# Column filtering in all chunks of layer 2 but the first of an image, with what makes room for it, in a two-layer convolution kernel

## The chip, the cores and the metric

The kernel runs on one core of a Trainium2 chip. The metric is the time of one execution on the device in microseconds (us); times of the kernel before are the median of three runs. The engines of the core are named as the profile names them: PE (TensorE; PEld are its weight loads), DVE (VectorE), ACT (ScalarE), POOL (GpSimd) and SP (SyncE, which here only issues transfers). Sixteen DMA engines move data; SP and ACT issue on hardware queues (q1 and q10 in the profile), POOL on a software queue (q0). L685 means line 685 of the kernel before.

## The reference

Two layers of the same form on x of shape (8, 32, 252, 252): group normalization (16 groups of two channels), a 5 by 5 convolution with reflect padding (written with FFTs), and the input added to it.

```
def _L0_conv_ref(x, weight):
    xp = jnp.pad(x, ((0, 0), (0, 0), (p, p), (p, p)), mode='reflect')
    wp = wp.at[:, :, :k, :k].set(weight)
    wp = jnp.roll(wp, shift=(shift, shift), axis=(-2, -1))
    out_fft = jnp.einsum('bihw,oihw->bohw', jnp.fft.fft2(xp), jnp.fft.fft2(wp))
    return jnp.fft.ifft2(out_fft).real[:, :, p:-p, p:-p]
...
x = x + _L0_conv_ref(_gn(x), L0_conv_weight)
x = x + _L1_conv_ref(_gn(x), L1_conv_weight)
```

The statistics of the second normalization are those of the first layer's whole image, so layer 2 of an image can begin only when layer 1 of it is done. All data are float32.

## The kernel before, in words

**Layout.** The 128 partitions hold 32 channels times two column parities times two row parities (`quad`), so that a 5 by 5 filter becomes a 3 by 3 filter over blocks of 2 by 2 pixels, and one 128 by 128 matrix product does all 32 channels and four parities at once. The residual addition is folded into the weights (`add_residual`), the normalization into weights and one bias.

**Row filtering (always).** Along rows a Winograd scheme is used: four output rows come from six "points". `transform` makes the inputs of the points on DVE: `v` holds sums of a row and the row two below (`row_pairs`, or for layer 2 `row_sums`, see below), `u` holds 4 times a row plus another (`row_quads`, `last_rows`); from `u` come points 2 and 1, from `v` points 4 and 3 and, with `points05` (L609), points 0 and 5. `conv` multiplies: each point takes three products of up to 128x508 (`product`, L685), one for each column tap. A float32 product shows as two records in the trace. Afterwards ACT and DVE combine the points (`seed`, `evacuate`, `first_pair`, `difference`, `inner`, `parts05`, `outer`): `inner` writes output rows 1 and 2 of each group of four to a tile y, and the "outer" rows 0 and 3 come from points 0 and 5.

**Column filtering (some chunks).** For points 0 and 5 the three products can be replaced by a second scheme along the columns: DVE makes sums and differences of neighbouring columns (`columns`, L618 to L628), PE does eight products of half the width (`column_product`, L707), ACT seeds one bank from another (`seed_columns`, L711), and DVE adds up (`column_parts`, L792 to L794). `by_columns` (L969) says which chunks do so: in layer 1 nearly all from image 1 on, in layer 2 chunks 1, 2, 3, 5 and 7 of images 0 to 5, chunks 1, 2, 3 of image 6 and 1 to 5 of image 7.

**Order of the work.** An image is eight chunks of 16 block rows. After the first image of layer 1 the list `order` takes in turn a chunk of layer 1 of image b + 1 and a chunk of layer 2 of image b; each has a slot of PE time. Where a chunk has no columns, its six products of points 0 and 5 are done in the next slot. Nothing is scheduled by a tool: each step is entered with a time in `at`, the table is sorted by these times, and each engine executes its instructions in that order. The times only set the order.

**Layer 2's inputs.** In layer 2 the sums v are made by transfers and not by DVE (`row_sums`, L557 to L560): POOL issues a copy of the chunk y to v (1032 KB), waits for it to land, and issues two accumulating transfers (903 KB and 129 KB) on the same queue. The tile v (tag "va") has one buffer, so the next copy waits until `points05` has read v.

**Other transfers.** SP loads chunks of x (`load`; most chunks are loaded for one column parity and copied on ACT by `even_columns`; the last chunk of an image and chunk 1 are loaded for both, four transfers of about 0.5 MB), loads pieces of the next image for its statistics (`load_piece`, two buffers, loaded two pieces ahead; ACT sums them in `piece_sums`, L235 and L241), and writes the output. For the output ACT first interleaves the two column parities from y into a tile o (`store`, L925), half a chunk at a time, then SP sends the rows (L910). Reflected border columns of layer 1's y are written by ACT (`reflect`, L869 to L872). POOL writes the borders of x (`borders`).

Of the kernel before, what the change touches and what calls it, by code (L numbers as in the profile page):

```python
# [42 lines left out]
F32 = mybir.dt.float32  # L43
# [6 lines left out]
P = 128  # L50
Q = 32
# [5 lines left out]
def tile_conv_preact_x2(ctx: ExitStack, tc: tile.TileContext, x: bass.AP, w0: bass.AP, w1: bass.AP, out: bass.AP):  # L57
# [17 lines left out]
    xpool = ctx.enter_context(tc.tile_pool(name="xpool", bufs=2))  # L75
    spool = ctx.enter_context(tc.tile_pool(name="spool", bufs=2))
    ypool = ctx.enter_context(tc.tile_pool(name="ypool", bufs=9))
# [167 lines left out]
    def load_piece(b: int, i: int):  # L245
        src = x[b].rearrange("ch h w -> (ch h w)").rearrange("(p n) -> p n", p=P)
        if b == 0:
            t = ypool.tile([P, PIECE], F32, tag="y", name=f"st_{b}_{i}")
        else:
            t = spool.tile([P, PIECE], F32, tag="st", name=f"st_{b}_{i}")  # L250
        parts = 3 if (b, i) == (0, NPIECE - 1) else 1
        m = PIECE // parts
        for j in range(parts):
            S.dma_start(t[:, j * m : (j + 1) * m], src[:, i * PIECE + j * m : i * PIECE + (j + 1) * m])
        pieces[b, i] = t
# [281 lines left out]
    def transform(t0: float, t1: float, b: int, l: int, c: int, free: float = -100.0, now=(0, 0, 0)):  # L537

        wi = WIN[l]
        got = {}  # L540
        sent = l == 1 and (b, c) != (0, 0)

        def source():
# [5 lines left out]
        def row_sums(add: bool):  # L549

            t, nxt = source()
            if not add:

                i = max(order.index((b, l, c)) - order.index((B - 2, 1, NCH - 2)), 0)
                got["v"] = vpool.tile([P, ROWS, wi], F32, tag=("va", "v")[i % 2], name=f"v_{b}_{l}_{c}")
                got["vt"] = got["v"].rearrange("p (t i) w -> p t i w", i=4)
                G.dma_start(got["v"], t)  # L557
            else:
                G.dma_start(got["v"][:, 0 : ROWS - 2], t[:, 2:ROWS], accum_op=ALU.add)  # L559
                G.dma_start(got["v"][:, ROWS - 2 : ROWS], nxt[:, 0:2], accum_op=ALU.add)  # L560

        def row_pairs(j0: int = 0, j1: int = NT):
# [49 lines left out]
        def columns():  # L612

            t, (m, mo) = ts[b, l, c][2], evens_odds(l)
            sd = vpool.tile([P, 2, NT, 2, m], F32, tag="sdiff", name=f"sdiff_{b}_{l}_{c}")
            d = tpool.tile([P, NT, 2, 2, m], F32, tag="t05", name=f"d05_{b}_{l}_{c}")
            odd, even = t[:, :, :, 1 : 2 * m : 2], t[:, :, :, 2 : 2 * m + 1 : 2]
            V.tensor_add(sd[:, 0], odd, even)  # L618
            V.tensor_sub(sd[:, 1], even, odd)
            if m == mo:  # L620
                f = "p t e (m a) -> p (t e) a m"
                V.tensor_sub(
                    d.rearrange("p t e a m -> p (t e) a m"),
                    t[:, :, :, 0 : 2 * m].rearrange(f, a=2), t[:, :, :, 2 : 2 * m + 2].rearrange(f, a=2),
                )
            else:
                V.tensor_sub(d[:, :, :, 0], t[:, :, :, 0 : 2 * m : 2], t[:, :, :, 2 : 2 * m + 1 : 2])
                V.tensor_sub(d[:, :, :, 1, 0:mo], odd[:, :, :, 0:mo], t[:, :, :, 3 : 2 * mo + 2 : 2])  # L628
            ts[b, l, c][2] = d, sd
# [14 lines left out]
        else:  # L644
            if sent:
                two = begin(order.index((b, l, c)) - 2)
                at(two + 1.45, row_sums, False)
                at(two + 8.4, row_sums, True)
            else:
                at(t0, row_pairs)  # L650
            for dt, fn in ((2, row_quads), (3.2, last_rows), (3.6, point2)):
                at(t0 + dt, fn)
            at(max(t0 + 4.2, free + 9.45) if sent else t0 + 4.2, point4)
# [7 lines left out]
    def conv(b: int, l: int, c: int, t0: float, t1: float, t2: float = 0.0, j0: int = 0, j1: int = NT, m05=None, later: float = 10.2):  # L661
# [28 lines left out]
        def half(tile_, i: int, e: slice, m: int):  # L690

            return tile_[:, e, i * nt * ne : i * nt * ne + nt * m].rearrange("p e (t w) -> p e t w", t=nt)

# [66 lines left out]
        def parts05():  # L760
# [3 lines left out]
            stt(to[1], sd[:, 2], 8.0, sd[:, 1], ALU.mult, ALU.add)  # L764

        def outer(e: int):

# [19 lines left out]
        def column_parts():  # L787
# [4 lines left out]
            V.tensor_add(half(sums05, 0, both, ne), m12, even)  # L792
            V.tensor_sub(odd, m2[:, :, :, 0:no], odd)
            V.tensor_sub(half(sums05, 1, both, no), odd, m12[:, :, :, 0:no])  # L794

# [20 lines left out]
        if columns:  # L816
# [6 lines left out]
            for i in range(2):  # L823
                at(t2 + 0.05, outer_columns, i)
        elif m05:
# [5 lines left out]
        else:  # L831
            at(t1 + 1.5, parts05)
            at(t2 + 0.05, outer, 0)
            at(t2 + 0.05, outer, 1)
        if nt < NT:
# [3 lines left out]
        else:  # L839
            store(t1 + 1.5 if m05 else t2 + 0.7, b, c, got)  # L840


    def keep(t1: float, t2, b: int, c: int, got):
# [18 lines left out]
        def reflect():  # L862
            lo, hi = (1 if c == 0 else 0), (ROWS - 1 if c == NCH - 1 else ROWS)
            y, copy, r = got["y"], A.copy, slice(lo, hi)

# [47 lines left out]

    def store(t0: float, b: int, c: int, got):

        end = (b, c) == (B - 1, NCH - 2)
        copy = V.tensor_copy if end else A.copy

        def interleave(h: int, s: int):
            if s == 0:  # L920
                pool, tag = (spool, "st") if end else (opool, "o")
                got["o", h] = pool.tile([P, 4, 2 * WOUT[1]], F32, tag=tag, name=f"o_{b}_{c}_{h}")
            r, m = 8 * h + 4 * s, (3 if (c, h, s) == (NCH - 1, 1, 1) else 4)
            for cp in range(2):
                copy(got["o", h][halves[s], 0:m, cp::2], got["y"][halves[cp], r : r + m, :])  # L925

        def send(h: int):
            got["o"] = got.pop(("o", h))
            for s in range(2):
                send_rows(b, c, h, s, got, (G, G) if end else (S, S))  # L930

        for i, t in enumerate((0, 3.3, 5.8, 7.8)):
            at(t0 + t, interleave, i // 2, i % 2)
        at(t0 + 4.6, send, 0)
        at(t0 + 9.1, send, 1)


    def store_half(t0: float, b: int, c: int, h: int, got):
        def interleave(s: int, rows: slice, engines):
            if (s, rows.start) == (0, 1):  # L940
                got["o"] = opool.tile([P, 4, 2 * WOUT[1]], F32, tag="o", name=f"o_{b}_{c}_{h}")
            for cp in range(2):
                dst, src = got["o"][halves[s], rows, cp::2], got["y"][halves[cp], 4 * s : 4 * s + 4][:, rows]
                eng = engines[cp]
# [24 lines left out]
    def by_columns(b: int, l: int, c: int) -> bool:  # L969
        if l == 0:  # L970
            return c < NCH - 1 and (b > 1 or (b == 1 and c > 1))
        return c in {B - 1: (1, 2, 3, 4, 5), B - 2: (1, 2, 3)}.get(b, (1, 2, 3, 5, 7))

# [62 lines left out]
    for i, (b, l, c) in enumerate(order):  # L1036
# [36 lines left out]
        if l == 0 and b + 1 < B:  # L1073
            wide = 1 if b == 0 else 2
            if c == 0:
                for j in range(2):
                    at(begin(i - 1) + 1.0 if b > 1 else t0 + (8.0 if b else 1.0), load_piece, b + 1, j)
            if c < NPIECE // 2:
                for j in range(2):
# [4 lines left out]
                    at(t, piece_sums, b + 1, p)  # L1084
                    if p + 2 < NPIECE:
                        at(t + 2.6, load_piece, b + 1, p + 2)
            if c == 2:
# [49 lines left out]
```

## Time and profile before

| | us |
|---|---|
| median of three runs (1878.82 to 1884.2) | 1880.79 |
| the profiled execution | 1879.27 |
| its span, first to last instruction | 1877.5 |
| PE busy | 1839.2 |
| DVE busy | 1731.2 |
| ACT busy | 1493.8 |
| POOL busy | 396.2 |
| an image in the steady stretch (846.4 to 1071.6 of the span) | 225.2 |

How to read the lines that follow. A line of the groups gives line, engine, operation, output and inputs, shapes, count, then total busy time and the mean duration in ns of one, then the idle time before them with who ended it. A line of the windows gives start and end of a stretch, its length, the busy time of PE, PEld, DVE, ACT and POOL in it (with the number of instructions), the clock granted to PE (1.00 is full), the busy share of the DMA engines and what they moved in GB/s. A line of a timeline gives start, duration, engine, line, operation and tiles, and in brackets idle time just before it and what ended that. A line of the chain gives start, length, and the engine and line. A line of the DMA issues gives the tiles, the queue, the count, the size of one and the median time from issue to landing. The granted clock was 0.994 over the execution.

### The profile page before, as it was taken

The page shows a single profiled execution, that of the slowest core. Times are in us where ns is not written, and L with a number is a line of the kernel's source. Part 1 is how long each engine was busy: PE and PEld are TensorE (multiplying, and loading weights), DVE is VectorE, ACT ScalarE, POOL GpSimd, SP SyncE. Part 2 cuts the span into 40 slices and gives each one's busy share as a digit, 9 for nine tenths or more (in the row PEclk, how much of TensorE's full clock was granted, in tenths as well). Part 3 has the DMA queues.
Part 4 walks back from the last instruction along what each step waited for, and adds up shares of the span by engine and source line. Part 5 has one row for each costly group of instructions (what it writes and reads, how often), then busy time and mean ns, then how long its engine had stood idle before and what let it go on. Part 6 is the DMA issues. An engine that isn't in the chain of part 4 may idle for free.

```text
span 1877.5 us, 20381 instructions
## 1 busy us (share of the span) xinstructions
PE 1839.2 (98%) x5194; PEld 966.0 (51%) x5194; DVE 1731.2 (92%) x3030; ACT 1493.8 (80%) x2781; POOL 396.2 (21%) x855
## 2 busy tenths in 40 slices
PE   5999999999999999999999999999999999999998
PEld 4444455545555555555555455554555555555455
DVE  7988799999999999999999899999999999997796
ACT  5886788878887888888898798987898876765575
POOL 4543111131112211122111311113111141110211
PEclk8999999999999999999999999999999999999999
DMA  9877578878888877987878967888878866775785
GB/s 275 203 179 180 151 209 199 210 194 202 217 202 219 194 209 192 221 223 173 220 193 206 235 175 205 205 204 204 212 202 198 214 165 140 179 174 148 195 212 125
DMA packets 207110, 369.07 MB, mean 197 GB/s; under 512 B 19088, under 2 KB 173968, under 8 KB 196752
## 3 DMA queue, kind: packets, MB, share of 16 engines
q1 hardware_dynamic: 178832, 230.73, 49.8%
q0 software_dynamic: 27600, 134.20, 29.3%
q10 hardware_dynamic: 560, 2.83, 0.4%
q8 instruction: 41, 0.67, 0.2%
q14 instruction: 77, 0.63, 0.1%
HBM read 167.15 MB, written 67.39 MB: 125 GB/s over the span
## 4 chain that ended last, share of the span: by engine, by line
PE 80%; DVE 7%; DMA 6%; ACT 3%; issue 3%; SPq 0%; POOL 0%; DVEq 0%; ACTq 0%; POOLq 0%
PE m L685 28%; PE pairs L685 28%; PE sums L707 7%; PE extra L707 6%; PE sums L685 6%; PE extra L685 4%; DMA v<-y 2%; DMA st<-in_x_dram 1%; DMA v<-ytail 1%; DMA xs<-in_x_dram 1%; ACT o L925 1%; DVE sd L748 1%; DVE t L609 1%; DMA wraw<-in_L_conv_weight_dram 1%; DMA out_dram<-o 0%
## 5 line engine op out<-in xcount | busy, mean ns | idle before, releaser
L685 PE MATMUL pairs<-t,u 128*128 128x504 f32 (+2 forms) x1548 | 692.9, 586 | 5.4 <-ACT pairs L729 3.3
L685 PE MATMUL m<-t,u 128*128 128x508 f32 (+3 forms) x1560 | 674.8, 581 | 3.4 <-DVE u L526 1.9
L685 PEld LDWEIGHTS m<-t,u 128*128 128x128 f32 x1560 | 294.2, 189 | 317.1 <-issue 297.0
L685 PEld LDWEIGHTS pairs<-t,u 128*128 128x128 f32 x1548 | 290.2, 189 | 320.1 <-issue 289.1
L925 ACT COPY o<-y 64x508 f32<-64x508 f32 x496 | 327.5, 660 | 8.6
L748 DVE SCALAR_TENSOR_TENSOR sd<-sd,pairs 128x504 f32<-128x504 f32 (+2 forms) x258 | 164.2, 671 | 19.5 <-PE pairs L685 15.2
L707 PEld LDWEIGHTS extra<-sdiff,wc 128*128 128x128 f32 x680 | 125.9, 189 | 98.1 <-issue 47.8
L707 PE MATMUL extra<-sdiff,wc 128*128 128x252 f32 (+3 forms) x680 | 173.0, 376 | 3.4 <-ACT extra L711 2.3
L860 ACT ACTIVATE junk<-y,negk 128x1008 bf16<-128x1008 f32 (+1 forms) x144 | 147.4, 1024 | 31.1 <-PE extra L707 14.5
L557 POOL DMA_DIRECT2D v<-y x63 | 35.7, 567 | 622.7 <-DVE t L609 608.4
L737 ACT COPY sd<-m 128x504 f32<-128x504 f32 (+2 forms) x258 | 136.9, 581 | 33.3 <-DVE sums L794 28.1
L609 DVE SCALAR_TENSOR_TENSOR t<-v 128x1024 f32<-128x1024 f32 (+1 forms) x128 | 157.7, 1232 | 5.4 <-PE sums L685 5.4
L707 PE MATMUL sums<-d,u 128*128 128x252 f32 (+3 forms) x680 | 157.4, 374 | 0.0
L707 PEld LDWEIGHTS sums<-d,u 128*128 128x128 f32 x680 | 127.6, 189 | 24.9 <-issue 9.0
L685 PE MATMUL sums<-t,u 128*128 128x508 f32 (+5 forms) x312 | 133.6, 577 | 0.0
L567 DVE TENSOR_TENSOR v<-xs 128x1792 f32<-128x1792 f32 (+1 forms) x65 | 130.2, 2003 | 1.2
L241 ACT ACTIVATE st<-st,negk 128x1134 f32<-128x1134 f32 x98 | 121.7, 1242 | 3.2
L559 POOL DMA_DIRECT2D v<-y x63 | 54.3, 862 | 329.1 <-DMA v<-y 329.1
L159 ACT COPY xs<-xs 64x1792 f32<-64x1792 f32 (+2 forms) x97 | 109.3, 1129 | 13.4 <-POOL xs L151 11.1
L729 ACT ACTIVATE pairs<-m,means 128x504 f32<-128x504 f32 (+1 forms) x129 | 84.2, 653 | 44.5 <-PE m L685 36.0
L785 ACT ACTIVATE y<-sums 128x504 f32<-128x504 f32 (+1 forms) x158 | 94.5, 634 | 28.3 <-PE sums L707 19.2
L235 ACT ACTIVATE st<-st 128x1134 f32<-128x1134 f32 x98 | 112.5, 1148 | 5.0 <-DMA st<-in_x_dram 3.2
(174 smaller groups left out, 2529.7 us busy)
## 6 DMA issues: line engine op xcount, KB each, us to landing
v<-y POOLq DMA_DIRECT2D x63, 1032.0 KB, 6.1
st<-in_x_dram SPq DMA_DIRECT2D x111, 567.0 KB, 6.1
out_dram<-o SPq DMA_DIRECT2D x480, 126.0 KB, 5.9
v<-y POOLq DMA_DIRECT2D x63, 903.0 KB, 7.7
xs<-in_x_dram SPq DMA_DIRECT2D x96, 441.0 KB, 8.4
xs<-in_x_dram SPq DMA_DIRECT2D x44, 504.0 KB, 12.0
u<-ud SPq DMA_DIRECT2D x15, 1152.0 KB, 6.0
xs<-in_x_dram SPq DMA_DIRECT2D x16, 472.5 KB, 9.3
```

The source lines that it names most:

```text
L159: copy(t[64:128, :, 0:256:2], t[0:64, :, 1:256:2])
L235: A.activation(junk, src, AF.Identity, accum_out=acc[:, 0, i : i + 1])
L241: A.activation(junk, src, AF.Square, bias=negk, accum_out=acc[:, 1, i : i + 1])
L567: (V.tensor_add if l else V.tensor_sub)(v[:, r0:r1], t[:, r0 + 2 : r1 + 2], t[:, r0:r1])
L609: stt(t, got["vt"][:, :, 0:2], 4.0 if l else -4.0, got["vt"][:, :, 2:4], ALU.mult, ALU.add)
L685: T.matmul(dst, u[:, k, 2 - i, :], rhs[:, j0 + i0 : j0 + i1, i : i + wo], start=(i == 0 and not add), stop=(i == 2), skip_group_check=add,)
L707: T.matmul(dst[:, 0, use], w, rhs[:, use], start=(i == 2), stop=True, skip_group_check=(i != 2))
L737: A.copy(got["sd"][:, 1 + e], m24[e][:, 0:n])
L748: stt(d, d, -2.0, pairs13[e][:, 0:n], ALU.mult, ALU.add)
L785: A.activation(y, src, AF.Copy, scale=1.0 - 2 * i, **total(3 * i))
L860: A.activation(dst, src, AF.Square, bias=negk, scale=1.0 if i else -1.0, accum_out=acc[:, 1, at_ : at_ + 1])
L925: copy(got["o", h][halves[s], 0:m, cp::2], got["y"][halves[cp], r : r + m, :])
```

## The change

Layer 2 uses column filtering in all chunks but the first of images 0 to 5, and in chunks 1 to 4 of image 6; this is 13 chunks more. With it come these edits:

- `u` of a layer-2 chunk that follows a layer-1 chunk (53 of 64 chunks) is no longer made by DVE: ACT writes four times the rows (`four_times`) and POOL issues three accumulating transfers (`outer_rows`) into a new tile with the tag "ua".
- Outer rows of layer 2 go from PSUM straight to an output tile (`outer_out`); `store` now treats outer and inner rows apart. The sign of the odd columns in `columns` and `column_parts` is turned for layer 2, and the layout of the odd half in PSUM (`half`) is padded.
- `reflect` runs on POOL but for chunks 0 and 7.
- `spool` has one buffer instead of two, and pieces for the statistics are loaded one ahead instead of two (image 1 apart).

```
-    spool = ctx.enter_context(tc.tile_pool(name="spool", bufs=2))
+    spool = ctx.enter_context(tc.tile_pool(name="spool", bufs=1))
...
+        sent_u = sent and order[order.index((b, l, c)) - 1][1] == 0
...
+        def four_times():
+
+            got["u"] = vpool.tile([P, 2, NT, wi], F32, tag="ua", name=f"ua_{b}_{l}_{c}")
+            src = source()[0].rearrange("p (t i) w -> p i t w", i=4)
+            A.activation(got["u"], src[:, 1:3], AF.Copy, scale=4.0)
+
+        def outer_rows():
+            t, nxt = source()
+            u1, u2 = got["u"][:, 0], got["u"][:, 1]
+            G.dma_start(u1, t[:, 3:ROWS:4], accum_op=ALU.add)
+            G.dma_start(u2[:, 0 : NT - 1], t[:, 4:ROWS:4], accum_op=ALU.add)
+            G.dma_start(u2[:, NT - 1], nxt[:, 0], accum_op=ALU.add)
...
                 at(two + 8.4, row_sums, True)
+                if sent_u:
+                    at(two + 5.3, four_times)
+                    at(two + 8.5, outer_rows)
             else:
                 at(t0, row_pairs)
-            for dt, fn in ((2, row_quads), (3.2, last_rows), (3.6, point2)):
-                at(t0 + dt, fn)
+            for dt, fn in ((2, row_quads), (3.2, last_rows)):
+                if not sent_u:
+                    at(t0 + dt, fn)
+            at(t0 + 3.6, point2)
...
+        def outer_out(e: int, engines):
+
+            if e == 0:
+                got["outer"] = out_tile(b, c, "outer")
+            t = slice(*tiles(5 * e))
+            for cp, eng in enumerate(engines):
+                to, bank = got["outer"][halves[e]], sums05[halves[cp], e]
+                if columns:
+                    dst = to.rearrange("p t (j i a) -> p t i j a", i=2, a=2)[:, t, :, :, cp]
+                    src = bank[:, 0 : 2 * nt * ne].rearrange("p (i t j) -> p t i j", i=2, t=nt)[:, t]
+                else:
+                    dst, src = to[:, t, cp : 2 * wo : 2], rows(bank[:, 0:n])[:, t]
+                (eng.copy if eng is A else eng.tensor_copy)(dst, src)
...
-            y, copy, r = got["y"], A.copy, slice(lo, hi)
+            y, copy, r = got["y"], A.copy if c in (0, NCH - 1) else G.tensor_copy, slice(lo, hi)
...
-        return c in {B - 1: (1, 2, 3, 4, 5), B - 2: (1, 2, 3)}.get(b, (1, 2, 3, 5, 7))
+        return c in {B - 1: (1, 2, 3, 4, 5), B - 2: (1, 2, 3, 4)}.get(b, (1, 2, 3, 4, 5, 6, 7))
...
-                for j in range(2):
-                    at(begin(i - 1) + 1.0 if b > 1 else t0 + (8.0 if b else 1.0), load_piece, b + 1, j)
+                for j in range(1 if b else 2):
+                    at(begin(i - 1) + 4.0 if b > 1 else t0 + (8.0 if b else 1.0), load_piece, b + 1, j)
...
-                    if p + 2 < NPIECE:
-                        at(t + 2.6, load_piece, b + 1, p + 2)
+                    ahead = 1 if b else 2
+                    if p + ahead < NPIECE:
+                        at(t + 2.6, load_piece, b + 1, p + ahead)
```

## The prediction

> **What bounds the kernel now.** I read the page first (busy time of the engines), then windows that cut the steady stretch into pairs of slots, then the chain that ended last, then the waits and the timelines of VectorE (DVE) and GpSimd (POOL) in two such pairs, then the DMA issues.
>
> ```profile
> PE 1839.2 (98%) x5194; PEld 966.0 (51%) x5194; DVE 1731.2 (92%) x3030; ACT 1493.8 (80%) x2781; POOL 396.2 (21%) x855
> q1 hardware_dynamic: 178832, 230.73, 49.8%
> q0 software_dynamic: 27600, 134.20, 29.3%
> HBM read 167.15 MB, written 67.39 MB: 125 GB/s over the span
> ```
>
> TensorE (PE) has work for 98% of the span. The next view holds pairs of slots of image 4 of layer 1 with image 3 of layer 2 (start and end, then busy times, clock, DMA share). The first two pairs have column filtering in both chunks; the third and the last begin and end around a chunk of layer 2 without it (chunks 4 and 6).
>
> ```profile
> 915.60:942.80 27.20, 27.20 (x81) 15.13 (x80) 26.89 (x44) 24.64 (x45) 3.36 (x9) 1.00 0.89 240
> 942.80:970.00 27.20, 27.20 (x81) 15.12 (x81) 26.89 (x43) 24.63 (x45) 3.25 (x9) 1.00 0.82 197
> 970.00:998.90 28.90, 28.90 (x78) 14.39 (x77) 25.97 (x44) 24.26 (x44) 4.49 (x10) 1.00 0.87 192
> 998.90:1026.20 27.30, 27.30 (x82) 15.17 (x81) 26.99 (x44) 22.23 (x42) 4.63 (x9) 1.00 0.87 237
> 1026.20:1058.90 32.70, 32.70 (x89) 15.91 (x88) 28.10 (x63) 26.36 (x49) 8.26 (x21) 1.00 0.83 200
> ```
>
> PE is full in each pair, DVE is at 26.89 of 27.20 in the pairs with columns, and the DMA engines are busy 82 to 89%. In the chain, the products of points 0 and 5 of a chunk without columns are one piece of 12 records; with columns they are eight short products:
>
> ```profile
> 990.60 0.85 PE extra L707 x4
> 993.14 0.85 PE extra L707 x4
> 993.99 5.11 PE sums L685 x12
> 1011.05 1.72 PE sums L707 x8
> ```
>
> So 5.11 us against 0.85 + 0.85 + 1.72 = 3.42: 1.7 us for each chunk, and 28.90 - 27.20 says the same.
>
> The third resource is a loop of transfers. A chunk of layer 2 gets v by a copy (L557) and two accumulating DMAs (L559, L560); the copy may start when DVE has read the v before it (L609). The timeline of POOL for chunk 3 and for chunk 5, the DMA issues of chunk 5 (the last figure is us to landing), and DVE at its end:
>
> ```profile
> 918.37 0.55 POOL L557 DMA_DIRECT2D v<-y  x1 [13.08 <-DVE t L609]
> 925.17 0.86 POOL L559 DMA_DIRECT2D v<-y  x1 [5.74 <-DMA v<-y]
> 946.60 0.55 POOL L557 DMA_DIRECT2D v<-y  x1 [13.02 <-DVE t L609]
> ...
> 974.83 0.55 POOL L557 DMA_DIRECT2D v<-y  x1 [12.08 <-DVE t L609]
> 981.56 0.86 POOL L559 DMA_DIRECT2D v<-y  x1 [5.67 <-DMA v<-y]
> ...
> v<-y POOLq DMA_DIRECT2D x1, 903.0 KB, 12.0
> v<-y POOLq DMA_DIRECT2D x1, 129.0 KB, 13.1
> ...
> 995.31 0.70 DVE L596 SCALAR_TENSOR_TENSOR t<-v 128x516 f32<-128x516 f32 x1 [2.62 <-DMA v<-y]
> ```
>
> In chunk 3 v has landed 15.6 us after its copy was issued and DVE reads it 6.3 us later. In chunk 5 it lands after 20.4 us, because four loads of 0.5 MB of xs were issued at 980 and the DMA share is 0.98 from 982 to 998.9; DVE waits 2.6 us for it. PE loses nothing, since this is the slot in which it has the 5.11 us of the chunk without columns.
>
> **The change, part by part.**
>
> *PE.* Thirteen more chunks by columns (chunks 4 and 6 of images 0 to 5, chunk 4 of image 6): 78 products of 128x508 go, 104 of half the width come. 13 x 1.7 = 22.1 us off, all on the path while PE is the bound.
>
> *DVE.* Each added chunk has four instructions of columns() (0.69 + 0.69 + 0.69 + 0.68) and three of column_parts() (0.70 + 0.68 + 0.69): 4.8 us, x 13 = 62.5. Against that 53 chunks lose row_quads and the u part of last_rows: 0.698 + 0.557 + 0.290 = 1.545, x 53 = 81.9. Net -19 us. A pair with columns comes to 26.9 - 1.5 = 25.4 of 27.2: by its work DVE would follow, with 1.8 us to spare in each pair.
>
> *ScalarE (ACT).* 120 copies fewer at about 0.65 (outer rows go from PSUM straight to the out tile): -78. Reflection goes to POOL: 192 x 0.22 = -43. four_times is new: 53 x 1.1 (the nearest rows are the 128x1008 square, 1.13, and the 128x1134 sum, 1.15) = +58; 13 seeds of 0.59 = +8. Net -55 us; ACT had 2.6 us free per pair, so I cost it at nothing: PE covers it, and if ACT were late the seeds (L729, L731) would hold PE.
>
> *Statistics tiles.* spool has one buffer instead of two and a piece is loaded one ahead. Between the end of the sums of one piece and the start of those of the next lie some 10 us; the median landing is 6.1 us and the odd pieces took 7 to 10. The cover is 0 to 4 us; if it is gone, ACT stands at L235 and the seeds behind it in its order wait. Bounds per image: 0 and two waits of 2 us; I take 0.
>
> *Writes of o.* Still 503 of up to 126 KB by SP, in the same rows of 1008 bytes: nothing. SP's order changes (a piece now waits for the sums before it, and the loads of xs stand behind it), hidden as long as xs is one chunk ahead.
>
> *POOL.* 192 small copies at 0.2 to 0.5 us and 159 DMA issues at 0.86 to 1.2 us: 396 us become 570 to 690, a third of the span. The reflected tiles are read a whole image later, so they cost nothing; but outer_rows stands between the v transfers and the next borders(), and its first issue waits for four_times. What lies behind that wait is the next chunk's borders, and behind those ACT's even_columns.
>
> *The u transfers, which decide it.* u is now four_times plus three accumulating DMAs, issued after those of v on the same queue: 128 x 8 rows of 516 bytes. No row has that size. In the trace's packets an accumulating one of 1032 bytes took 104 ns and one of 7224 bytes 565; the line through both gives 66 ns for 516 bytes. Bounds: half the small one (52) and all of it (104): 1024 packets over 16 engines are 3.3 to 6.7 us; I take 66 ns, 4.2 us, since the line uses both rows. The gain has no lower bound below 3.3, as the queue carries more in any case.
>
> point2 is DVE's first instruction for the chunk and needs u, where before only point4 needed v. From the start of point2 to the end of L609 DVE took 939.00 to 946.30 = 7.3 us, and 0.3 to the next copy. So the loop is: landing of v + 4.2 + 7.6, once per pair of slots. With the landings of image 3 of layer 2 before:
>
> - chunk 1: 19.0 + 11.8 = 30.8 against slots of 28.7: 2.1 late
> - chunk 2: 13.3 + 11.8 = 25.1 against 27.2: gives it back
> - chunks 3 and 4: 15.6 and 15.3: 27.4 and 27.1 against 27.2: even
> - chunk 5: 20.4 + 11.8 = 32.2 against 27.2 (28.9 before): 5.0 late
> - chunk 6: between 15.6 (as chunk 3) and 20.0 (as before): 0.2 to 4.6 late
> - chunk 7: 20.7 + 11.8 = 32.5 against 32.7 - 1.7 = 31.0: 1.5 late
> - chunk 0 of the next image: 14.0 + 11.8 = 25.8 against some 26: even
>
> In chunk 3 point2 ended at 939.7 and PE needs it at 942.8, so about 2.5 us of lateness are free (3.1 less what the next steps leave). Lateness of chunk 1 fits in that; of chunks 5 to 7, 6.7 to 11.1 less 2.5 leave 4.2 to 8.6 us per image.
>
> To it comes the load itself. An image of 225.2 us has a DMA share of 0.83, 188 us; eight times 4.2 more are 222, in a period that PE would make 222. All landings get longer. Bound: nothing, or some 1 us in each pair whose loop is even, 3 us per image. I take 7.5 us per image for both, the upper middle, since a share near 1.0 is nearest to the row of 982 to 998.9, where an accumulation took 12.0 us instead of 7.3. Six images have the full load (image 6 runs beside no piece loads): 6 x 7.5 = 45.
>
> *Sum.* The profiled execution took 1879.3 us, of which the span is 1877.5; the median shown is 1.5 above it. 1879.3 - 22.1 + 45 = 1902.2; on the median, 1904.
>
> **A rule against the row.** The row is the DMA share of 0.83 and the 0.98 between 982 and 998.9 at 191 GB/s. The Trainium skill, Perfetto Trace Analysis, "Identifying the Most-Contended Engine", says to judge DMA by the use of HBM and not by occupancy; "Engine Utilization" there gives 358 GB/s as a core's peak. By it 197 GB/s is 55%, transfers have room, and the sum would be 1857 on the profiled execution. I go by the row, since v landed late there.
>
> **Rivals.**
> 1. *The transfers stay covered.* For it: DVE has 1.8 us more in each pair, v had 6 us of slack in chunks 2 to 4, and u's small packets may go between those of xs. Against it: u comes after v, and is wanted before it. Decides if the landing of u in chunk 5 stays below 22 us after the copy. 1880.8 - 22.1 = 1859: faster, the other side.
> 2. *DMA becomes the bound.* 222 us of packets at a share of 0.95 are a period of 234 per image instead of 225: +8.8, and with bubbles 12: over 6.5 images +57 to +78, 1938 to 1959. For it: the shares of 0.98. Against: packets are shorter when fewer queue up.
> 3. *It cancels.* 3.7 us per image are lost: 1875 to 1886.
>
> **How the numbers follow.** The late loop 0.42 (1887 to 1930, itself 1904), covered 0.30, DMA-bound 0.20, cancelled 0.08. A measurement of this kernel tells some 0.3% from no change (1875.1 to 1886.4). Faster 0.31, same 0.07, slower 0.62. The range leaves out a little of the best end and most of the DMA-bound case's upper half: 1857 to 1946; the likeliest case's own is 1887 to 1930.
>
> **What would show it.** PE's busy time near 1817, chunks 4 and 6 of layer 2 with L707 products in place of their L685. DVE's longest wait at point2 (on DMA ua), 2 to 6 us, in chunks 5 to 7; POOL's wait for DMA v<-y above 329 us; a DMA share of 0.90 or more over an image and pairs of 28 to 33 us. If DVE does not wait at point2, rival 1 holds and I am wrong in the 4.2 us or in the order on the queue; if ACT waits at L235 instead, I am wrong in the statistics tiles.

## The result, and where the profile after shows the time

The kernel after takes 2128.9 us (2125.3 to 2136.6) against 1879.8 for the kernel before, each the median of four runs: a ratio of 1.133, 95% interval 1.129 to 1.137. It is slower by 249 us; the prediction said 24 us. In the profiled execution the span is 2129.2 us.

The page of the kernel after:

```profile
PE 1888.1 (89%) x5246; PEld 991.6 (47%) x5246; DVE 1713.0 (80%) x2960; ACT 1527.6 (72%) x2535; POOL 632.8 (30%) x1206
HBM read 167.15 MB, written 67.39 MB: 110 GB/s over the span
PE 33%; DMA 19%; ACT 14%; DVE 13%; issue 12%; SPq 4%; POOL 2%; ACTq 0%; DVEq 0%; POOLq 0%
L798 ACT COPY o_outer<-sums 64x512 f32<-64x512 f32 (+1 forms) x242 | 238.8, 987 | 56.5 <-DMA out_dram<-o_inner 19.7
L235 ACT ACTIVATE st<-st 128x1134 f32<-128x1134 f32 x98 | 112.5, 1148 | 149.7 <-DMA st<-in_x_dram 149.2
```

No engine is full any more: PE works for 89% of the span instead of 98%. In the chain that ended last PE has a third, and DMA, ACT and DVE share most of the rest. ACT stood 149 us at L235 for a piece of the statistics; in the kernel before it was 3 us.

Windows of the kernel after (columns as in the prediction): slots of chunk 5 of layer 1 and chunk 5 of layer 2, and a whole image.

```profile
1114.20:1127.70 13.50, 13.50 (x41) 7.51 (x40) 13.25 (x23) 7.87 (x15) 1.76 (x5) 1.00 1.13 185
1127.70:1158.50 30.80, 16.98 (x42) 8.64 (x42) 14.75 (x24) 16.97 (x25) 8.30 (x12) 0.72 0.73 168
962.10:1224.90 262.80, 233.04 (x645) 123.07 (x645) 213.33 (x362) 198.01 (x329) 79.70 (x142) 0.94 0.85 192
```

An image takes 262.8 us instead of 225.2. The slot of layer 2's chunk 5 takes 30.8 where the kernel before has 13.7. Over the seven images this one slot accounts for some 111 of the 249 us; the rest is spread over the other slots. The next three views say why this slot is long; they are the timelines of SP, ACT and PE.

```profile
1111.13 6.16 SPq L143 DMA_DIRECT2D xs<-in_x_dram  x6
1117.33 11.53 SPq L143 DMA_DIRECT2D xtail<-in_x_dram  x8
1128.90 1.88 SPq L986 DMA_DIRECT2D out_dram<-o_inner  x4
1130.88 10.35 SPq L255 DMA_DIRECT2D st<-in_x_dram  x2
```

```profile
1138.24 1.15 ACT L235 ACTIVATE st<-st 128x1134 f32<-128x1134 f32 x1 [13.89 <-DMA st<-in_x_dram]
...
1141.87 4.23 ACT L798 COPY o_outer<-sums 64x512 f32<-64x512 f32 x4
1146.12 0.66 ACT L749 ACTIVATE pairs<-m,means 128x508 f32<-128x508 f32 x1
```

```profile
1127.74 5.27 PE L705 MATMUL m<-t,u 128*128 128x508 f32 x12
1146.83 6.64 PE L705 MATMUL pairs<-t,u 128*128 128x508 f32 x8 [13.82 <-ACT pairs L749]
```

SP spends 18 us on the 14 loads of an image's last chunk (xs and xtail). Behind them stand the writes of `o_inner` and the load of the next piece, which could be issued only at 1130.9, long after its tile was free (the sums before it ended at 1113). ACT waits 13.9 us for it; behind it in ACT's order stand four direct copies of 1.06 us and the seed (L749) that PE needs. PE idles 13.8 us, and then runs at a lower clock: the granted clock is 0.50 from 1146.8 to 1150.0 and 1.00 again from 1153.4, and the eight records at 1146.83 take 6.64 us where the eight of the slot before took 3.54. The granted mean of this slot is 0.72 and PE's busy time is 17.0 us instead of 13.7.

In the kernel before SP spends as long on the same loads, but no engine stands waiting for what comes behind them:

```profile
980.03 3.15 SPq L143 DMA_DIRECT2D xs<-in_x_dram  x6
983.23 14.90 SPq L143 DMA_DIRECT2D xtail<-in_x_dram  x8
```

### The profile page after: what moved, and what is told of

Read it like the earlier page. It is cut to its first block, busy times and chain, and to the rows that moved or that the text cites. A ratio compares the mean times of both kernels' runs of the same rounds, so it can differ in the third digit from the quotient of the medians.

```text
span 2129.2 us, 20725 instructions
## 1 busy us (share of the span) xinstructions
PE 1888.1 (89%) x5246; PEld 991.6 (47%) x5246; DVE 1713.0 (80%) x2960; ACT 1527.6 (72%) x2535; POOL 632.8 (30%) x1206
## 3 DMA queue, kind: packets, MB, share of 16 engines
HBM read 167.15 MB, written 67.39 MB: 110 GB/s over the span
## 4 chain that ended last, share of the span: by engine, by line
PE 33%; DMA 19%; ACT 14%; DVE 13%; issue 12%; SPq 4%; POOL 2%; ACTq 0%; DVEq 0%; POOLq 0%
PE pairs L705 15%; PE m L705 8%; ACT o_outer L798 7%; DMA st<-in_x_dram 6%; DMA xs<-in_x_dram 4%; PE extra L705 3%; DMA ua<-y 3%; DMA v<-y 3%; SPq L143 3%; PE extra L727 2%; PE sums L727 2%; DMA out_dram<-o_inner 2%; ACT junk L904 2%; ACT st L235 2%; DVE sd L768 1%
## 5 line engine op out<-in xcount | busy, mean ns | idle before, releaser
L705 PE MATMUL pairs<-t,u 128*128 128x504 f32 (+2 forms) x1548 | 751.5, 625 | 172.7 <-ACT pairs L749 160.7
L705 PEld LDWEIGHTS pairs<-t,u 128*128 128x128 f32 x1548 | 305.3, 202 | 528.6 <-issue 310.0
L798 ACT COPY o_outer<-sums 64x512 f32<-64x512 f32 (+1 forms) x242 | 238.8, 987 | 56.5 <-DMA out_dram<-o_inner 19.7
L826 DVE TENSOR_TENSOR sums<-extra,sd 128x512 f32<-128x512 f32 (+1 forms) x98 | 68.0, 694 | 229.8 <-ACT o_outer L798 228.9
L235 ACT ACTIVATE st<-st 128x1134 f32<-128x1134 f32 x98 | 112.5, 1148 | 149.7 <-DMA st<-in_x_dram 149.2
L727 PE MATMUL extra<-sdiff,wc 128*128 128x256 f32 (+3 forms) x784 | 201.2, 377 | 12.4 <-DVE sdiff L634 7.2
L727 PEld LDWEIGHTS extra<-sdiff,wc 128*128 128x128 f32 x784 | 145.0, 189 | 123.0 <-issue 72.6
L727 PE MATMUL sums<-d,u 128*128 128x252 f32 (+3 forms) x784 | 182.2, 375 | 0.0
L978 ACT COPY o_inner<-y 64x508 f32<-64x508 f32 x248 | 164.1, 662 | 5.5 <-DMA out_dram<-o_outer 3.6
L624 DVE SCALAR_TENSOR_TENSOR t<-v 128x1024 f32<-128x1024 f32 (+1 forms) x128 | 158.1, 1235 | 4.4 <-PE sums L705 4.4
L727 PEld LDWEIGHTS sums<-d,u 128*128 128x128 f32 x784 | 146.7, 189 | 21.9 <-issue 1.9
L561 POOL DMA_DIRECT2D v<-y x63 | 53.6, 851 | 328.2 <-DMA v<-y 323.6
L148 POOL COPY xs<-xs 64x4 f32<-64x4 f32 (+3 forms) x113 | 44.0, 389 | 318.1 <-DMA xs<-in_x_dram 265.4
L749 ACT ACTIVATE pairs<-m,means 128x504 f32<-128x504 f32 (+1 forms) x129 | 84.3, 653 | 56.8 <-PE m L705 54.8
```

The lines of the kernel that those rows point to most:

```text
L235: A.activation(junk, src, AF.Identity, accum_out=acc[:, 0, i : i + 1])
L624: stt(t, got["vt"][:, :, 0:2], 4.0 if l else -4.0, got["vt"][:, :, 2:4], ALU.mult, ALU.add)
L705: T.matmul(dst, u[:, k, 2 - i, :], rhs[:, j0 + i0 : j0 + i1, i : i + wo], start=(i == 0 and not add), stop=(i == 2), skip_group_check=add,)
L727: T.matmul(dst[:, 0, use], w, rhs[:, use], start=(i == 2), stop=True, skip_group_check=(i != 2))
L749: A.activation(dst, src, AF.Identity, bias=norm[b, l][1][:, 0:1])
L798: (eng.copy if eng is A else eng.tensor_copy)(dst, src)
```

## The experiments

A slot is counted from the start of its first product of point 2 to that of the next slot. Each kernel was compared with the kernel before on the same chip, which gave 1877 to 1880 us there. The expectations weigh theories against each other: S is the single statistics tile, U the transfers of u, O the direct copies, C the added columns; later L is the length of a direct copy, W the writes of the o tile, D VectorE's wait for u and B the load that u's making and its transfers put on the rest.

### First split of the kernel after

**Pieces loaded by ACT.**

```
- S.dma_start(t[:, j * m : (j + 1) * m], ...)
+ (A if b > 1 else S).dma_start(t[:, j * m : (j + 1) * m], ...)
- at(t + 2.6, load_piece, b + 1, p + ahead)
+ at(t + (0.0 if b else 2.6), load_piece, b + 1, p + ahead)
```

> The kernel after, but the loads of the pieces of images 2 to 7 are issued by ACT itself, directly behind the sums of the piece before, instead of by SP. Buffer, bytes and sums stay the same. Theory S (the single statistics tile: its load stands in SP's order behind loads of xs and writes of o, and SP itself stands until ACT has summed the piece before): ACT's wait at L235, 149 us, falls below 60 and the time to 1930 to 2010. Theory U (the transfers of u, as the prediction had it): 2110 to 2140, ACT's wait may fall but VectorE still waits for ua. Theory O (the copies of L798, 1.07 us each, hold the bank of the sums): 2080 to 2130.

Measured 2094.5 us (2085.8 and 2103.3), 34 below the kernel after. The wait at L235 fell from 149 to 8 us as theory S said, but the time did not follow. The lateness went one instruction further: ACT now waits at L798 for a free o tile.

```profile
ACT o_outer L798 <- DMA out_dram<-o_inner: 107.9, 14, 13.7
```

(Columns of a wait: total us, times, longest.) In the kernel after this wait was 19.7 us. The o tile is freed by the writes of `o_inner`, and these too stand behind the 14 loads on SP. Two things wait for the same late SP, and taking one away shows the other.

**u by VectorE; then also two tiles.**

```
- sent_u = sent and order[order.index((b, l, c)) - 1][1] == 0
+ sent_u = False
```

and for the second run in addition `spool` with two buffers and pieces loaded two ahead, as in the kernel before.

> The kernel after with u made by VectorE again (row_quads and last_rows): four_times and the three accumulating transfers of u are gone, the statistics tile stays single. Theory U: 1880 to 1960, at most some 50 us above the time before. Theory S: VectorE loses its 52 us of waits for ua but gets 82 us of work, the wait of ACT at L235 stays above 100 us, 2070 to 2130. Theory O: the same as S.

> As the run with u by VectorE, and the statistics pieces have two tiles again and are loaded two ahead. The difference to that run is the second tile alone. Theory S: 100 to 200 us faster than that run, 1900 to 1960. Theory U: within 15 us of that run. Theory O: within 30 us of that run, and both above 2050.

Measured 2068.4 and 2021.7 us: the transfers of u cost 60.5, the second tile gives back 46.7. Neither is the whole, and 142 us remain without either. So neither theory S nor U is sufficient; 2068 lies just below what S and O said of the first run and far above U, and 2022 of the second run fits none of the three. S also had the wait at L235 above 100 us in the first run; it was 89. In the run with two tiles ACT waits at the direct copies (timeline of ACT, then of SP):

```profile
1076.49 4.24 ACT L798 COPY o_outer<-sums 64x512 f32<-64x512 f32 x4 [6.17 <-DMA out_dram<-o_inner]
```

```profile
1060.62 11.68 SPq L143 DMA_DIRECT2D xtail<-in_x_dram  x8
1072.34 1.86 SPq L986 DMA_DIRECT2D out_dram<-o_inner  x4
```

**Outer rows by y.** In chunks with columns, the rows go from the bank to y in two copies and from y to o in four, as in the kernel before; once in the kernel after, once in the run with u by VectorE and two tiles.

```
- at(t2 + 0.05, outer_out, i, (A, A))      # chunks with columns of layer 2
+ at(t2 + 0.05, outer_columns, i)
- store(..., b, c, got, m05 is not None)
+ store(..., b, c, got, m05 is not None or columns)
```

> The kernel after, but in layer 2's chunks with columns the outer rows go through y again: two copies from the bank of the sums to y and four from y to o, instead of four strided copies from the bank to o. Theory O: the bank is free some 3 us earlier in each of 49 chunks, VectorE's wait at L826 for L798 (229 us) goes, 1980 to 2050. Theory S: ACT's work is about the same (2 x 0.7 + 4 x 0.65 = 4.0 us against 4 x 1.07 = 4.3), the wait at L235 stays, within 40 us of the time after. Theory U: within 20 us.

> The run with u by VectorE and two statistics tiles (2021.7), and in layer 2's chunks with columns the outer rows go through y again. Theory O (the direct copies: 4.3 us of ACT stand ahead of the seeds and hold the bank, and wait for a free o tile behind the writes): 1880 to 1930. Theory C (the added columns, VectorE being full): 1980 to 2020, L798 was only where the lateness showed. Theory R (order of the writes on SP by outer and inner rows): 1980 to 2030.

In the kernel after: 2285.2 us, 156 slower, against every expectation. Without u's transfers and with two tiles: 1928.6, which is 93 below the same run with direct copies and in theory O's range. The first result has its own line among the waits:

```profile
DVE y L777 <- DMA ua<-y: 314.0, 29, 15.5
```

There are nine y tiles. In this run `inner` of layer 2 (L777) is given a tile that the transfers for the next chunk are still reading: at 1143.0 of the span it starts after 15.5 us of idle time, just after the second of the transfers of u that were issued at 1126 to 1128 has landed (1142.9). In the kernel after, with direct copies, no instruction at L777 idles for as much as 0.2 us. A likely reason is that outer rows which pass through y hold layer 2's y longer, so that no other tile is free; no run shows it (one with a tenth tile would). So the direct copies are what lets u be sent without this wait, and at the same time they cost 93 us.

### Each part alone, put into the kernel before

```
- return c in {... B - 2: (1, 2, 3)}.get(b, (1, 2, 3, 5, 7))            # columns alone
+ return c in {... B - 2: (1, 2, 3, 4)}.get(b, (1, 2, 3, 4, 5, 6, 7))
- spool = ... bufs=2                                                     # one tile
+ spool = ... bufs=1       # and load_piece one ahead instead of two
+ at(two + 5.3, four_times); at(two + 8.5, outer_rows)                   # one tile, u sent
```

> The kernel before with the list of chunks with columns of the kernel after, nothing else: 13 chunks more. PE gets 22.1 us less work, VectorE 62.5 us more, 4.8 us in pairs where it was at 25.97 of 28.90. Theory C: VectorE bounds these pairs at some 31 us: 1895 to 1935. Theory O or S: 1860 to 1890, the columns are not what costs.

> The kernel before with one statistics tile, loaded one piece ahead, nothing else. Theory S (the single tile costs by itself): 1920 to 1970, the 47 us between the two runs with u by VectorE. Rival: it costs only where the direct copies and the writes already hold ACT and SP: below 1890.

> The kernel before with one statistics tile and with u by ACT and transfers, nothing else. The difference to the run with one tile alone is the price of the transfers of u. Theory U as the prediction had it: 45 us (up to 60) above that run. Rival: 53 x 1.5 us of VectorE fall away in a kernel whose pairs leave VectorE 0.3 us, and the transfers of u hide: 0 to 15 us above or below it.

Columns alone: 1924.6 us, 44.7 slower (ratio 1.0235, interval 1.020 to 1.027), as theory C said of the time. Windows of that run, the pairs of slots that begin with chunks 4 and 6 of layer 2:

```profile
993.90:1022.00 28.10, 27.79 (x82) 14.96 (x81) 27.79 (x46) 24.68 (x45) 3.28 (x7) 1.00 0.87 182
1050.30:1086.40 36.10, 33.05 (x94) 17.22 (x93) 33.03 (x69) 26.58 (x49) 8.43 (x20) 0.95 0.75 159
```

The first pair gains 0.8 us (28.9 before), DVE now being busy for 27.8 of 28.1; theory C had some 31 for it. The pair between the two loses 1.0 (28.3 instead of 27.3). The second pair shown loses 3.4 (32.7 before): DVE's work rose from 28.1 to 33.0. In it VectorE works without a gap from 1049.5 to 1072.5, and PE idles 2.9 us until VectorE has the statistics of the image (L336) ready, so PE's share is no longer what sets the pair.

One tile alone: 1957.2 us, 77 slower, as theory S said, and more than the 47 of the second tile above. Most of it is in the slot of layer 2's chunk 5, 22.7 to 26.7 us instead of 13.7 in images 3 to 5, with the same wait (total us, times, longest):

```profile
ACT st L235 <- DMA st<-in_x_dram: 120.2, 24, 16.2
```

One tile and u sent: 2325.8 us, 369 above the run before it. Again it is `inner` and its y tile, and neither theory had named it. In the run with one tile alone, `inner` of layer 2 waits in the same place for ACT (by the semaphores in its trace) and does not idle; with u sent it waits for the transfers of the next chunk, 16.8 us at 949:

```profile
DVE y L777 <- DMA ua<-y: 436.6, 39, 17.3
```

### What makes the direct copies dear

```
- dst = to.rearrange("p t (j i a) -> p t i j a", i=2, a=2)[:, t, :, :, cp]              # plain copies
+ dst = to[:, :, cp * 128 : cp * 128 + 128].rearrange("p t (i j) -> p t i j", i=2)[:, t]
- at(t0 + 9.5, load, ...)                                                               # writes first
+ at(t0 + 9.9, load, ...)
```

> The run with u by VectorE and two tiles (2021.7), in which the four direct copies of a chunk with columns write 128 neighbouring values of the o tile instead of every fourth one; the outer rows of these chunks then have their columns in the wrong order, the count, the source and the written bytes are the same. Theory L (a copy is slow because of its scattered destination, and the 4.3 us ahead of the seeds cost 1.1 us in each slot): a copy falls to 0.65 to 0.85 us, slots of layer 2 from 14.7 to about 13.9, and 30 to 60 us go: 1960 to 1990. Theory W (ACT waits for a free o tile, behind writes that stand behind loads): the slots of chunk 5 stay at 22 to 24 us, at most 25 us go: 1997 to 2022.

> The same run (2021.7) with one change of order on SP: the loads of a chunk of xs stand behind the four writes of o_inner of that slot instead of ahead of them (entered at 9.9 instead of 9.5). Theory W: ACT's wait at L798 for the write of o_inner, 62 us, falls below 20, slots of chunk 5 from 22 to 24 to 14 to 16, 40 to 60 us go: 1960 to 1980. Theory L: within 15 us of 2021.7.

Both were made from the run with u by VectorE and two tiles (2021.7). The kernel with plain copies leaves the columns of these outer rows in the wrong order; it serves to time the copies alone. Plain copies: 1958.1 us, 64 below; writes first: 1977.8, 44 below. Both theories were right about their part, and L by a little more than it said. With the writes first, the slot of chunk 5 went from 22 to 24 us down to 14.3, and the wait at L798 for the write from 62.3 to 26.4 (W had said below 20); the other slots of layer 2 stayed at 14.5 to 14.8. With plain copies it was the other way round: most slots of layer 2 back at 13.67, chunk 5 still at 19 to 21.

The third run is made from the one with the writes first. It keeps the result and changes only the order in which a copy steps:

```
- dst = to.rearrange("p t (j i a) -> p t i j a", ...)   src = ... "p (i t j) -> p t i j"
+ dst = to.rearrange("p t (j i a) -> p t j i a", ...)   src = ... "p (i t j) -> p t j i"
```

> The run with u by VectorE, two tiles and the writes ahead of the loads (1977.8); the four direct copies step through the o tile in the order of its columns (inner step of two values, and the source jumps) instead of one half of the columns after the other (inner step of four values, the source in order). Result and bytes are the same. If a copy is long because of its scattered destination: below 0.85 us each and 1925 to 1950, which would account for all 93 us together with the order on SP. If it is long whatever the order: 1.0 us or more, 1965 to 1990.

Measured 1935.7 us, 42 below the run it was made from. The two changes together take away 86 of the 93 us. The group of the copies in the kernel after, with plain copies, and in row order (count, then total us and mean ns of one):

```profile
L798 ACT COPY o_outer<-sums 64x512 f32<-64x512 f32 x192 | 205.6, 1071 | 31.0 <-DMA out_dram<-o_inner 13.8 <-PE sums L727 12.6 <-issue 2.3
```

```profile
L798 ACT COPY o_outer<-sums 64x512 f32<-64x512 f32 x192 | 110.8, 577 | 61.7 <-DMA out_dram<-o_inner 48.7 <-PE sums L727 8.5 <-issue 2.3
```

```profile
L798 ACT COPY o_outer<-sums 64x512 f32<-64x512 f32 x192 | 120.0, 625 | 25.5 <-DMA out_dram<-o_inner 17.9 <-PE sums L727 3.0 <-issue 2.3
```

A copy whose destination steps 16 bytes takes 1071 ns; the same elements in an order that steps 8 bytes, with a source that jumps instead, 625; a plain one 577. The Trainium skill, ScalarE: Activation LUTs, "What ACT_TABLE_LOAD costs", gives 186 ns and 0.833 ns an element for an ACTIVATE with immediate scale and bias. Taken for these copies of 512 elements that makes an estimate of 613 ns; it has no term for the step of the destination, and it comes near the last two and not the first.

### What the transfers of u cost

> The kernel after with four_times and the three accumulating transfers of u left in place into the tile ua, which nobody reads; VectorE makes its own u as before and uses that. Against the run with u by VectorE (2068.4) it adds the transfers and ACT's work, against the kernel after (2128.9) it takes away VectorE's wait for ua. Theory D (the prediction's loop: u lands late and VectorE waits): 2060 to 2085. Theory B (the transfers and four_times cost by their load and by holding y and POOL): 2110 to 2150.

> The run with u sent and not used (2119.7) without the three accumulating transfers: only ACT's four_times into ua remains (53 of 1.07 us, 57 us of ACT). Against the run with u by VectorE and one tile (2068.4). If ACT's work is what costs: 2105 to 2125. If the transfers cost: 2065 to 2085. Between them both do.

Both are made from the kernel after. The first has u sent into a tile that nobody reads, and VectorE makes its own u; the second leaves out the three transfers as well and keeps `four_times`. Measured 2119.7 and 2064.3 us. Against the kernel after, VectorE's wait for u, less the work that it is spared, is worth 9 us, no more than the runs of the kernel after differ among themselves (2125 to 2137); the transfers themselves are worth 55, `four_times` nothing that shows (2068.4 without it). Theory D falls, B holds, and within B it is not ACT. The wait for the piece, with and without the transfers:

```profile
ACT st L235 <- DMA st<-in_x_dram: 146.5, 31, 15.2
```

```profile
ACT st L235 <- DMA st<-in_x_dram: 89.3, 19, 13.8
```

The transfers make the pieces later by 57 us of ACT's waiting; that these are the same 55 us is likely, but it was not tried separately.

### Mending the order

```
- ... 4.0 if early else 9.5), load, ...          # writes first and pieces by ACT
+ ... 4.0 if early else 9.9), load, ...
- at(t1 + (0.2 if early else 9.0), borders, ...) # borders of the last chunk behind v
+ at(t1 + (0.2 if early else (23.0 if part[0] else 15.1) if kc == NCH - 1 and nb > 1 else 9.0), borders, ...)
```

> The kernel after with both changes of order: the writes of o_inner ahead of the loads of xs, and the pieces of images 2 to 7 loaded by ACT. All of its transfers, tiles and columns remain. If order on SP is what its lateness comes from: 1960 to 2010, u's transfers leaving VectorE's waits at L607 (52 us in the kernel after). If the single tiles and the load itself limit: 2050 to 2095, as with the pieces by ACT alone (2094.5).

> The run with both changes of order (2147.3), with one more: on POOL the borders of an image's last chunk stand behind the copy of v of layer 2's chunk 6, those of its tail behind u's transfers, instead of ahead of both. If POOL standing there is what makes u late in chunk 6 (VectorE's waits at L607, 251 us): waits below 120, slot of chunk 6 of layer 1 from 28 to 14 to 18, 2040 to 2085. If the transfers themselves are too slow: within 25 us of 2147.

Writes first and pieces by ACT: 2147.3 us, 53 slower than the pieces by ACT alone, against both expectations. Chunk 5 of layer 2 is mended (15.3 us), but chunk 6 of layer 1 takes 28 to 29 instead of 13.6, and here the prediction's wait appears. Waits, then the timeline of POOL:

```profile
DVE t L607 <- DMA ua<-y: 251.3, 43, 18.6
```

```profile
1160.50 0.19 POOL L153 COPY xtail<-xtail 64x2 f32<-64x2 f32 x1 [11.54 <-DMA xtail<-in_x_dram]
...
1161.12 0.57 POOL L559 DMA_DIRECT2D v<-y  x1 [0.31 <-DVE sd L783]
```

The loads, pushed behind the writes, land later; POOL stands at their borders until 1160.7, and v and u of the next chunk of layer 2 stand behind. With the borders moved: 2090.4 us, 57 less, chunk 6 at 16.6. The place was right; the time is just above the range (2040 to 2085) and the waits at L607 fell only to 178 instead of below 120.

> The kernel after with the four direct copies in the order of the o tile's columns, nothing else. The copies fall from 1.07 to about 0.62, 88 us of ACT in all. If the parts add up (the copies' length was 42 to 64 of the 93 us): 2045 to 2090. If the late pieces and the writes at chunk 5 hide it: 2105 to 2130.

> The run with writes first, pieces by ACT and the borders moved (2090.4), and the copies in the order of the columns: everything of the kernel after but its four sources of delay. If the transfers of u keep pace once nothing else is late: 1890 to 1950. If they are late by themselves (VectorE's waits at L607 stay at 100 us or more): 2000 to 2070.

The kernel after with copies in row order and nothing else: 2094.2 us, 35 less, just outside what adding up allowed, since chunk 5 (27 to 29 us) still waits for its piece: the wait at L235 is 173 us. With everything mended: 2071.4, 1 us above the range for transfers that are late by themselves. Here the transfers of u bound most pairs: ACT's wait at L235 is down to 8 us and that at L798 for a free o tile to 14, while VectorE waits 37 times at L607 for ua, 179.6 us in all. Timelines of DVE and POOL of this run around two chunks of layer 2:

```profile
1050.81 0.70 DVE L607 TENSOR_TENSOR t<-ua 128x516 f32<-128x516 f32 x1 [4.10 <-DMA ua<-y]
...
1081.85 0.69 DVE L607 TENSOR_TENSOR t<-ua 128x516 f32<-128x516 f32 x1 [4.32 <-PE sums L727]
...
1087.91 1.23 DVE L624 SCALAR_TENSOR_TENSOR t<-v 128x1032 f32<-128x1032 f32 x1
...
1113.74 0.70 DVE L607 TENSOR_TENSOR t<-ua 128x516 f32<-128x516 f32 x1 [5.19 <-DMA ua<-y]
```

```profile
1058.40 0.57 POOL L559 DMA_DIRECT2D v<-y  x1 [10.68 <-DVE t L624]
...
1066.03 2.66 POOL L575 DMA_DIRECT2D ua<-y  x1
...
1089.44 0.57 POOL L559 DMA_DIRECT2D v<-y  x1 [10.91 <-DVE t L624]
```

From copy to copy 31.04 us, against a pair of PE's of 27.2. The last transfer of u, issued at 1066.0, lands 15.7 us later at 1081.7 (the DMA issues of this window); DVE starts point2 at 1081.85, is through L624 at 1089.1, and POOL issues the next copy at 1089.4. (The profile puts the middle wait to PE, whose products end at 1081.8 too; the waits before and after it are put to ua.) This is the prediction's loop, at 23.4 + 7.6 us. The last piece of v landed at 1073.9 by the same view, so u adds 7.9 us to v, not 4.2. In these 7.9 us the packets of u held 45% of the DMA engines' time, and those of 1008 bytes, the loads of x, 48%.

### Columns in chunk 4 only

```
- return c in {... B - 2: (1, 2, 3)}.get(b, (1, 2, 3, 5, 7))
+ return c in {... B - 2: (1, 2, 3, 4)}.get(b, (1, 2, 3, 4, 5, 7))
```

> The kernel before with columns in chunk 4 too (7 chunks more instead of 13; chunk 6 stays without). In the run with all 13 the pair of chunk 4 took 28.0 against 28.9 us and the pair of chunk 6 36.5 against 32.7. If the columns cost only where VectorE has its long slot of an image's end: 1870 to 1882, at best 6 us faster than before. If VectorE, full in each pair with columns, falls behind in chunk 5 already: 1885 to 1900.

Measured 1891.2 us (ratio 1.0057, interval 1.004 to 1.007): slower by 11. The pair of chunk 4 gains 0.9 us as in the run with all 13, but the next pair takes 28.2 to 28.4 instead of 27.2, and the long slot of layer 1's chunk 7 mostly loses 1 to 3.5. No version tried beats the kernel before.

### The sum

Along one path each step is one change, and the steps add up to the whole by construction: before 1879.9; columns +44.7; the rest of the change in its place (reflection on POOL, the o tiles and writes by inner and outer rows, direct copies in the chunks without columns) +4.0; direct copies in the chunks with columns +93.1; one statistics tile +46.7; u sent +60.5; after 2128.9. On another path a step can have another size (one tile alone in the kernel before cost 77).

## Why the prediction was wrong

The direction was right, the size was not, and the likeliest case was the wrong one. By the path above, the columns cost 44.7 us where their products were to save 22.1, the direct copies 93.1 and the single tile 46.7 where nothing was costed, and the transfers of u 60.5 where 45 was. That the forecast went the right way owes little to its reason, the late loop of u, which hardly shows in the kernel after.

- *PE, −22.1.* The products came out as said, but their saving was not on the path. In the run with the columns alone a pair gained 0.8 us where 1.7 was costed, and others lost. PE's busy time is 1888 us, not 1817; part of that is the clock, whose granted mean fell from 0.994 to 0.950.
- *DVE, −19 net.* Measured −18.2 (1713.0 against 1731.2). "By its work DVE would follow" was not tested in the kernel after, where DVE is held up elsewhere; with u on DVE the columns cost 45, and VectorE falls behind in the pairs that begin with chunks 5 and 6.
- *ACT, −55 net, "I cost it at nothing: PE covers it".* This step failed first. ACT's work rose by 34 us. The term at fault is the direct copy, costed at about 0.65 us as that of a row: it takes 1.07 in chunks with columns, so 192 copies are 81 us more. And cover was judged by the free time in a pair, although the copies stand ahead of the seed in ACT's order, hold the bank of the sums for 4.2 us instead of 1.3, and wait for a free o tile. The prediction named the seeds as what would be held, and did not price it.
- *Statistics tiles, "0 and two waits of 2 us; I take 0".* This failed second: 47 to 77 us. The cover was worked out from the landing time. What counted was when SP could issue the load, behind 14 loads; one wait of 13 to 15 us per image and a few of 1 to 5, not two of 2. The text had named this wait as what would prove it wrong.
- *Writes of o, "nothing".* This failed third: the order on SP is worth 44 us with direct copies. The reason given, xs one chunk ahead, looked at the loads and not at what waits for the writes. In the kernel before the same 14 loads hold SP for 18 us (980.0 to 998.1 in its timeline), and nothing there waited for it long: 8.6 us of idle time stand before all of ACT's copies to o, 3.2 us of waits for pieces at L235.
- *POOL.* 633 us of work, inside 570 to 690. No run tries it alone; the step that holds the reflection cost 4.0 us. Where loads got later, POOL standing at borders cost 57 us.
- *The u transfers, 45 us.* The price was near (60; 55 of it without any reader), but that is luck, since the mechanism was not the one at work: the wait of VectorE, net of its spared work, is worth 9 us. The runs show in its place that the transfers make the pieces late, by 57 us of ACT's waiting. The packet was right, 66 ns against a median of 67 and a mean of 72.7 in the trace after. The landing was not: 4.2 us were 7.9 in the mended run, where the loads of x held as much of the engines' time as u did. The loop itself is real and became the bound once the rest was mended.
- *What would show it.* DMA share of an image 0.85, not 0.90; POOL's wait for v 323.6, not above 329. VectorE's longest wait at point2 was 7.6 us, and not the cause.
- *The rule.* The prediction set 197 GB/s against the page's peak, but that is all that the DMA engines moved; the page speaks of HBM, and there the kernel before moved 125 GB/s and the kernel after 110. The Trainium skill, Perfetto Trace Analysis, "Identifying the Most-Contended Engine", has DMA judged by the use of HBM before one looks for the DMA resource that binds. By the 358 GB/s of its section "Engine Utilization", 110 is an estimated 31%. The transfers of u run within SBUF and do not show in it (167.15 MB read before and after), and yet the run with unread transfers is 55 us slower than the one without. The use of HBM gave no sign of this; the lateness of single transfers did.

## What to carry to other kernels

When an intermediate tile is taken out between an accumulator bank and an output, the bank and its producer begin to wait for the output's writes: follow the write back through its queue before costing the copy. A buffer's cover runs from the moment its load can be issued, not from the moment the buffer is free; read what stands ahead of it on the issuing engine in the worst slot of the period, not in the median one. When several things wait for the same late queue, removing one moves the lateness to the next, so measure the parts alone and along one path.

## What the runs showed of the hardware that was not expected

- ACT's copies of 64x512 from PSUM took 1071, 625 and 577 ns for destination steps of 16 bytes, 8 bytes and 4 bytes (inner step).
- In the trace SP's transfers use eight semaphores in turn, and each issue waits on the one used eight issues before. In the last chunk's 14 loads the gaps of 1.3 to 2.2 us between single issues fall on such waits: 32 rows of 1008 bytes stand behind half a megabyte. In the run with writes first and pieces by ACT the eight small loads took 23 us to issue.
- After an idle stretch of 13.8 us PE's granted clock was 0.50 when the products went on, and 1.00 again some 6 us later. The slot's products took 3.3 us longer than in a slot without such a stretch.
